# Attention with a routed expert gate: half of the projections placed in attention's first four chunks, and the gate cut into 128-token pieces

## The chip, the cores and the metric

One core of a Trainium2 chip runs the whole kernel in one launch. The metric is the device time in microseconds (us). Engines are named as in the profile: PE is TensorE (PEld its weight loads), DVE is VectorE, ACT is ScalarE, POOL is GpSimd, SP is SyncE, which here only issues transfers and waits. All data is float32.

## The reference

The input x has 2 batches of 2048 tokens with 256 features, 4096 tokens in all. It is normalised once, and both branches read the normalised rows.

```python
xn = layernorm(x)
# attention branch: 16 heads of 16, relative positions clipped to +-128
q, k, v = (heads(xn @ W.T + b) for W, b in ((Wq, bq), (Wk, bk), (Wv, bv)))
scores  = (q @ k.T + q . rel_k[clip(j - i, -128, 128) + 128]) / sqrt(16)
w       = softmax(scores)
s       = (w @ v + w . rel_v[clip(...) + 128]) @ Wo.T + bo
# expert branch: 8 experts (256 -> 1024 -> 256), one chosen for each token
e       = argmax(xn @ Wg + bg)
g       = silu(gelu(xn @ W1[e]) @ W2[e])
out     = x + s * g
```

## The kernel before

The work is done in three stages that follow each other on every engine; the order of the instructions within a stage is that of the source (`manual_schedule`), and a scheduler may place an instruction of a later stage earlier on an engine whose turn it is (loads of the attention stage stand among those of the expert stage on SP, for instance).

**Stage 1, up to 157 us: normalisation, routing, projections.** The tokens come in 8 blocks of 512 (`TB`, `NI = 8`). For each block, x is loaded, normalised on DVE, stored row-wise (`xn_d`, for the experts' gathers), and transposed on PE into `xnT`, which holds all 4096 tokens with the features on the partitions. `logits` multiplies by the router's weights. The projections are a list of 56 `pieces`, 7 per block: two of `queries` and two of `keys` (`project`, L272: two 128x512 products, an ACT activation that adds the bias, and a store to `q_d` or `k_d`), one `right_rows` (L294: the extra query row for keys beyond the right clip, from the products of the two q tiles, stored in `qx_d`), and two of `values_of` (L306: four 128x256 products, two DVE additions of the bias `bvl` into a buffer `vt` whose other columns hold ones, and a store to `v_d` after the second half). `right_rows` also stores a block of zeros `zq` into the other row of `qx_d` (L304). `work_pieces(n)` takes the next n pieces from the list; the calls stand where PE would wait for the normalisation (1 per block) and for the routing tables on DVE (2, and 13 at L496), and the rest, 30 and 3, at L523 and L542. Between the two the pieces are followed by L525 to L541, which need small loads that POOL issues at L507 to L512 (wo_t, relk_t, rvc, ones_r): ones are copied into the two key buffers, `into` is built, and L534 multiplies it with wo_t. Routing ends with `token` (L502): the list of tokens by expert, after which POOL gathers the rows of the first two tiles (`get_tokens`, L156) and SP loads the weights of the first two (`get_weights`, L143, L147).

**Stage 2, 157 to 430 us: the experts.** 19 tiles of 256 sorted tokens (`work`, L552): transposes, `hp` products (L583), gelu on ACT, `yp` products (L598), a store to `ys_d`. Weights and gathered rows are double-buffered.

**Stage 3, from 431 us: attention.** There are 2 batches x 4 groups of 4 heads x 16 chunks of 128 queries = 128 chunks; four chunks make a unit. Chunk n runs in `steps` of a written-out loop (L1093 to L1180). In each step PE gets score products: the band (keys within one chunk, `band_scores` L785), the relative scores of two later chunks (`rel_scores` L745), and the far keys of the unit before (`far_scores` L940), which exist from chunk 4 on. All of these take their PSUM tile from the pool `sps` with 5 buffers in turn; a drain (DVE for band and relative scores, ACT's exponential for far keys) frees it. After the drains come the "small" tasks that `at(k, ...)` has put into step k. The ones that matter here:

- `to_keys(n + 1)`, step 0: DVE L772, then on SP a store of the relative scores to DRAM (`qr_d`, L776) and a load back in skewed form (`r`, L778, 768 KB each). The band drains of chunk n + 1 (L801) read r; the last of them is followed by L813, one reduction per chunk, which I use as the chunk's mark.
- `band_weights(n - 1)`, steps 0 and 1: exponentials on ACT in r (L824), then on POOL a store to `w_d` (L837) and a load `wr` (L839).
- `turn_rel`, `turn_band`, `band_values`: transposes and products of the band's weights.
- `load_q`, `load_kv`: loads for the next unit (L657, L660) and the next head group (L670, L678), on SP.
- `gate(i, 0)` in step 3 of chunks 2 to 9: four indirect gathers (L692, POOL) bring the expert results of 512 tokens; `gate(i, 1)` in step 2 of chunks 4 to 11: tanh on ACT (L701), two POOL operations (L702, L703), and a store of the gate to `gate_d` on SP (L704).

SP is one queue in order: an instruction that waits holds everything behind it. So are POOL's and ACT's queues.

Of the kernel before, what the change touches and what calls it, by code (L numbers as in the profile page):

```python
# [8 lines left out]
F32 = mybir.dt.float32  # L9
I32 = mybir.dt.int32  # L10
AF = mybir.ActivationFunctionType
ALU = mybir.AluOpType
# [22 lines left out]
def attn_moe_gate_kernel(  # L35
# [60 lines left out]
    NI = T // TB  # L96

    xn_d = dram.tile([T, D], F32, name="xn_d")
    gate_d = dram.tile([P, NT * D], F32, name="gate_d")
    ys_d = dram.tile([NE * TE, D], F32, name="ys_d")  # L100
    q_d = dram.tile([D, T], F32, name="q_d")
# [6 lines left out]
    def load(name, shape, src, pool=const):  # L108
        t = pool.tile(shape, F32, name=name)
        nc.gpsimd.dma_start(out=t, in_=src)  # L110
        return t
# [9 lines left out]
    token = const.tile([P, NB], I32, name="token")  # L121
    expert = const.tile([P, NE], I32, name="expert")
    filled = const.tile([P, 1], I32, name="filled")
    vdiff = const.tile([P, 1], F32, name="vdiff")
    rel0 = const.tile([P, 1], F32, name="rel0")

# [9 lines left out]

    feeding = ExitStack()
    feed = feeding.enter_context(tc.tile_pool(name="feed", bufs=2, side="right"))

    def get_weights(i, pool):  # L140
        e = nc.sync.value_load(expert[0:1, i : i + 1], min_val=0, max_val=E - 1)
# [23 lines left out]
    with ExitStack() as own:  # L165
# [31 lines left out]
        for e in range(E):  # L197
            nc.vector.memset(rank[:, e : e + 1], float(E - e))
        wq_t = load("wq_t", [P, ND, D], wq.rearrange("(k p) m -> p k m", p=P), ln1)
        bq_t = load("bq_t", [P, ND], bq, ln1)  # L200
        wk_t = load("wk_t", [P, ND, D], wk.rearrange("(k p) m -> p k m", p=P), ln1)
        bk_t = load("bk_t", [P, ND], bk, ln1)
        rkc = load("rkc", [P, 2], relk_cols, ln1)
        wv_t = load("wv_t", [P, ND, D], wv.rearrange("(k p) m -> p k m", p=P), ln1)
        bvl = load("bvl", [P, HEADS, HD], bv.partition_broadcast(P), ln1)
# [50 lines left out]
        def logits(i):  # L256
            for t in range(i * CB, (i + 1) * CB):
                for k in range(ND):
                    nc.tensor.matmul(
                        plog[:, t, :],  # L260
                        lhsT=xnT[:, k, t * P : (t + 1) * P],
                        rhs=wg_t[:, k, :],
                        start=(k == 0),
                        stop=(k == ND - 1),
                    )

        qx_heads = qx_d.rearrange("(h two) t -> h two t", two=2)
        rights, qs = [], {}  # L270

        def project(i, w, a, bias, scale, dst, name):  # L272
            cols = slice(i * TB, (i + 1) * TB)
# [20 lines left out]
        def right_rows(i):  # L294
            cols = slice(i * TB, (i + 1) * TB)
            ps = pps.tile([HEADS, TB], F32, name="pp")
            for a in range(ND):
                nc.tensor.matmul(
                    ps, lhsT=rights[a], rhs=qs.pop((i, a)), start=(a == 0), stop=(a == ND - 1)
                )  # L300
            rt = prp.tile([HEADS, TB], F32, name="rt")
            nc.scalar.copy(rt, ps)
            nc.sync.dma_start(out=qx_heads[:, 1, cols], in_=rt)
            nc.sync.dma_start(out=qx_heads[:, 0, cols], in_=zq)  # L304

        def values_of(i, half):  # L306
            vt = vts[i % 2]
# [22 lines left out]


        pieces, later = [], []
        for i in range(NI):
            pieces += [(queries, i, 0), (queries, i, 1), (keys, i, 0), (keys, i, 1)]
            pieces.append((right_rows, i))
            later += [(values_of, i, 0), (values_of, i, 1)]
            if not 0 < i < 3:
                pieces, later = pieces + later, []

        def work_pieces(n):  # L340
            for what, *args in pieces[:n]:
                what(*args)
            del pieces[:n]

        take_stats(0)
        for i in range(NI):
            if i + 6 < NI:
                get_x(i + 6)
            if i + 1 < NI:
                take_stats(i + 1)  # L350
            normalise(i)
            if i == 0:
                nc.vector.tensor_scalar(bq_t, bq_t, HD**-0.5, None, ALU.mult)
                nc.vector.tensor_scalar(bk_t, bk_t, rkc[:, 0:1], None, ALU.add)

                nc.vector.tensor_tensor(
                    right, rkc[:, 1:2].to_broadcast([P, HEADS]),
                    rkc[:, 0:1].to_broadcast([P, HEADS]), ALU.subtract,
                )
                for a in range(ND):  # L360
                    r = ln1.tile([P, HEADS], F32, name=f"right{a}")
                    nc.gpsimd.affine_select(
                        out=r, in_=right, compare_op=ALU.is_ge, fill=0.0, base=a * P,
                        pattern=[[-HD, HEADS]], channel_multiplier=1,
                    )
                    nc.gpsimd.affine_select(
                        out=r, in_=r, compare_op=ALU.is_ge, fill=0.0, base=HD - 1 - a * P,
                        pattern=[[HD, HEADS]], channel_multiplier=-1,
                    )
                    rights.append(r)  # L370
                nc.gpsimd.memset(before, 1.0)
                nc.gpsimd.affine_select(
                    out=before, in_=before, compare_op=ALU.is_ge, fill=0.0, base=-1,
                    pattern=[[1, P]], channel_multiplier=-1,
                )
                nc.gpsimd.memset(ones, 1.0)
                nc.gpsimd.memset(zq, 0.0)
                nc.gpsimd.iota(
                    begin, pattern=[[TE, NE]], base=0, channel_multiplier=0,
                    allow_small_or_imprecise_dtypes=True,  # L380
                )
                nc.gpsimd.iota(place, pattern=[[1, P]], base=0, channel_multiplier=0)
                nc.gpsimd.iota(number, pattern=[[P, NT]], base=0, channel_multiplier=1)
                for vt in vts:
                    nc.gpsimd.memset(vt, 1.0)
            if i == 1:
                nc.vector.tensor_tensor(
                    bvl, bvl, rve[:, 0:1, :].to_broadcast([P, HEADS, HD]), ALU.add
                )
            if i > 0:  # L390
                logits(i - 1)
                work_pieces(1)
        logits(NI - 1)
        work_pieces(1)
        lnx.close()


# [122 lines left out]
        nc.gpsimd.memset(mass[:, MASS : MASS + 1], 1.0)  # L520
        for z in shifts:
            nc.gpsimd.memset(z, 0.0)
        work_pieces(len(pieces) - 3)  # L523
        for t in k_homes:
            nc.vector.tensor_copy(t, ones_r.to_broadcast([P, S]))  # L525

# [99 lines left out]
            _attention(own, again)  # L626

    def _attention(own, again):
        accp = own.enter_context(tc.tile_pool(name="sacc", bufs=1))
        gop = own.enter_context(tc.tile_pool(name="gout", bufs=2))  # L630
        gpp = own.enter_context(tc.tile_pool(name="gprod", bufs=1))
        kvp = own.enter_context(tc.tile_pool(name="kv", bufs=2))
        qrp = own.enter_context(tc.tile_pool(name="qr", bufs=2))
        rp = own.enter_context(tc.tile_pool(name="r", bufs=3))
        bandp = own.enter_context(tc.tile_pool(name="band", bufs=2))
        wrtp = own.enter_context(tc.tile_pool(name="wrt", bufs=1))
        smp = own.enter_context(tc.tile_pool(name="small", bufs=2))
        exps = own.enter_context(tc.tile_pool(name="exps", bufs=18))
        finp = own.enter_context(tc.tile_pool(name="fin", bufs=2))
        outp = own.enter_context(tc.tile_pool(name="outp", bufs=2))  # L640
        scr = own.enter_context(tc.tile_pool(name="scr", bufs=3, space=DRAM))
        sps = own.enter_context(tc.tile_pool(name="sps", bufs=5, space=PSUM))
        avps = own.enter_context(tc.tile_pool(name="avps", bufs=1, space=PSUM))
# [38 lines left out]
            groups[G] = {"kT": kT, "v": v}  # L682


        gates = {}

        def gate(i, stage):
            if stage == 0:
                yt = gates[i] = gop.tile([P, CB * D], F32, name="yt")
                for c in range(CB):  # L690
                    t = i * CB + c
                    nc.gpsimd.indirect_dma_start(  # L692
                        out=yt[:, c * D : (c + 1) * D],
                        out_offset=None,
                        in_=ys_d,
                        in_offset=bass.IndirectOffsetOnAxis(ap=slot[:, t : t + 1], axis=0),
                    )
                return
            yt = gates.pop(i)
            gt = gpp.tile([P, CB * D], F32, name="gt2")  # L700
            nc.scalar.activation(gt, yt, AF.Tanh, scale=0.5)  # L701
            nc.gpsimd.tensor_scalar(gt, gt, 0.5, 0.5, ALU.mult, ALU.add)  # L702
            nc.gpsimd.tensor_tensor(gt, gt, yt, ALU.mult)  # L703
            nc.sync.dma_start(out=gate_d[:, i * CB * D : (i + 1) * CB * D], in_=gt)  # L704


        def chunk_of(n):
# [352 lines left out]

        load_q(0)
        load_kv(0)
        for drain in [rel_scores(0, j) for j in range(HG)]:
            drain()
        to_keys(0)
# [27 lines left out]
        while n < NCH or values or any(queues) or n <= NCH + 2 * CB + 1:  # L1093
# [26 lines left out]
            if live and m == 6 and (G + 1) * NC < NCH:  # L1120
                at(0, load_kv, G + 1)
            if not again:
                if 2 <= n < 2 + T // TB:
                    at(3, gate, n - 2, 0)
                if 4 <= n < 4 + T // TB:
                    at(2, gate, n - 4, 1)
            Uf, stage = divmod(n - 2, CB)
            if 0 <= Uf - 2 < NU:
                at(0, finish, Uf - 2, stage)
# [11 lines left out]
            if 0 <= n - 1 < NCH:  # L1141
                for part in range(1, chunk_of(n - 1)["f1"] - chunk_of(n - 1)["f0"]):
                    at(min(4, steps - 1), turn_band, n - 1, part)
            for k in range(steps):
                drains, filled = [], []
                for j in range(HG):
# [122 lines left out]
```

## Time and profile before

| what | us |
|---|---|
| three runs | 2314.58, 2300.74, 2314.71 (median 2314.58) |
| the profiled execution | 2314.34 |
| its span, first to last instruction | 2312.6 |
| routing table `token` done (L502) | 95.85 |
| last projection piece / first expert product (L583) | 153.63 / 158.84 |
| end of the experts on PE / start of attention on PE | 429.43 / 431.44 |
| first product with far keys (L946), the start of chunk 4 | 491.64 |
| L813 of chunk 4 / 12 / 20 / 28 | 497.13 / 629.28 / 740.15 / 849.71 |

The profile's page gives busy time per engine, forty equal slices of the span (57.8 us each) with PE's granted clock, the costliest groups of instructions, and the transfers. In a timeline each row is a start, a length, and an instruction with its line and tiles; what stands in brackets is the idle time before it and what ended it. In the windows each row is a stretch, its length, the busy time and count on PE, PEld, DVE, ACT and POOL, the clock that PE was granted (1.00 is full speed), the share of the DMA engines in use, and GB/s. In a list of waits each row is a sum in us, how many times, and the longest.

### The profile page before, as it was taken

The numbers are of one execution on the slowest core, as the hardware profiler recorded it, in microseconds if no ns is written. First come the engines' busy times: TensorE is split into PE (matmuls) and PEld (weight loads), VectorE is DVE, ScalarE is ACT, GpSimd is POOL, SyncE is SP. The second block draws the span as 40 slices with busy tenths as digits, with TensorE's granted clock in tenths as the row PEclk, the third lists the DMA queues.
The fourth block names the chain that finished last, engine by engine and source line by source line (L and its number), as shares of the span: only waits on it lengthen the run. The fifth ranks groups of instructions, "written<-read, shape, count | busy, mean of one in ns | idle before, by whom it ended". The sixth has DMA issues, their size and how long they took to land. (4 is left out here: it accounts for less than half of the span.)

```text
span 2312.6 us, 58344 instructions
## 1 busy us (share of the span) xinstructions
PE 2204.5 (95%) x24314; PEld 1435.4 (62%) x24314; DVE 1065.3 (46%) x2688; ACT 1294.2 (56%) x2519; POOL 426.7 (18%) x587
## 2 busy tenths in 40 slices
PE   7999999788999999999999998899999999999996
PEld 5568888655565566666566565566556656656653
DVE  5421000244555555555455554455555555555542
ACT  2221111146666676666676666566667666666664
POOL 1201110045311111111111222211111111111221
PEclk9999999779999999999999999899999999999998
DMA  5646555477666766766676667566666666666652
GB/s 182 217 170 182 184 183 181 136 255 254 224 224 207 237 217 208 241 223 204 213 232 228 230 231 227 195 210 218 225 205 218 219 213 219 216 213 218 239 189 71
DMA packets 246802, 483.16 MB, mean 209 GB/s; under 512 B 16480, under 2 KB 194944, under 8 KB 246016
## 3 DMA queue, kind: packets, MB, share of 16 engines
q1 hardware_dynamic: 199648, 295.21, 38.8%
q0 software_dynamic: 41008, 178.84, 22.7%
q10 hardware_dynamic: 5872, 5.26, 0.7%
q8 instruction: 195, 3.19, 0.6%
q14 instruction: 79, 0.65, 0.1%
HBM read 244.89 MB, written 234.36 MB: 207 GB/s over the span
## 5 line engine op out<-in xcount | busy, mean ns | idle before, releaser
L956 ACT ACTIVATE ex<-sp 128x512 f32<-128x512 f32 x1728 | 893.3, 587 | 540.6 <-PE sp L946 420.9
L946 PE MATMUL sp<-qh,kT 32*128 32x512 f32 (+7 forms) x4096 | 766.0, 559 | 28.7 <-DVE stat L801 28.4
L801 DVE CUSTOM_DVE_ANT_0 r<-sp,r 128x384 f32<-128x384 f32 (+1 forms) x512 | 275.6, 539 | 615.7 <-PE sp L946 331.9
L791 PE MATMUL sp<-kT,qh 31*128 31x384 f32 (+1 forms) x1024 | 457.7, 533 | 0.0
L946 PEld LDWEIGHTS sp<-qh,kT 32*128 32x128 f32 (+1 forms) x4096 | 297.6, 184 | 220.7 <-issue 134.6
L966 PE MATMUL av<-ex,v 128*17 128x256 f32 (+2 forms) x7168 | 422.3, 371 | 0.0
L753 PE MATMUL sp<-relk_t,qh 32*128 32x256 f32 x1024 | 291.5, 412 | 13.8 <-DVE stat L801 10.8
L966 PEld LDWEIGHTS av<-ex,v 128*17 128x17 f32 (+1 forms) x7168 | 195.4, 99 | 173.6 <-issue 65.3
L824 ACT ACTIVATE r<-r,shift 128x384 f32<-128x384 f32 (+1 forms) x512 | 282.9, 613 | 10.0 <-DVE shift L813 10.0
L867 DVE COPY wt<-mp 128x512 f32<-128x512 f32 x368 | 242.6, 684 | 11.3 <-PE mp L865 6.2
L865 PEld LDWEIGHTS mp<-ident,r 128*128 128x128 f32 x1472 | 158.6, 142 | 143.0 <-issue 130.6
L839 POOL DMA_DIRECT2D wr<-w_d x128 | 97.8, 764 | 725.7 <-PE sp L946 167.0
L865 PE MATMUL mp<-ident,r 128*128 128x128 f32 x1472 | 220.4, 285 | 0.5 <-ACT r L824 0.5
L762 DVE COPY qr<-sp 128x512 f32<-128x512 f32 x256 | 175.4, 686 | 43.3 <-PE sp L946 34.7
L753 PEld LDWEIGHTS sp<-relk_t,qh 32*128 32x128 f32 x1024 | 172.2, 190 | 27.4 <-DVE stat L801 11.9
L888 PE MATMUL mp<-ident,wr 128*128 128x128 f32 x1024 | 157.9, 277 | 26.7 <-DVE qh L851 13.8
L837 POOL DMA_DIRECT2D w_d<-r x128 | 71.7, 560 | 514.3 <-ACT r L824 504.4
L590 ACT ACTIVATE hT<-hp 128x512 f32<-128x512 f32 x76 | 45.3, 597 | 215.7 <-PE hp L583 215.7
L791 PEld LDWEIGHTS sp<-kT,qh 31*128 31x128 f32 x1024 | 152.6, 187 | 4.0 <-issue 2.1
L888 PEld LDWEIGHTS mp<-ident,wr 128*128 128x128 f32 x1024 | 119.7, 142 | 48.8 <-DVE qh L851 25.9
L583 PE MATMUL hp<-xsT,w_t 128*128 128x256 f32 x608 | 134.4, 379 | 1.1 <-issue 1.1
L598 PE MATMUL yp<-w_t,hT 128*128 128x256 f32 x608 | 134.4, 379 | 0.0
(177 smaller groups left out, 1992.9 us busy)
## 6 DMA issues: line engine op xcount, KB each, us to landing
qr_d<-qr SPq DMA_DIRECT2D x128, 768.0 KB
r<-qr_d SPq DMA_DIRECT2D x128, 768.0 KB
w_d<-r POOLq DMA_DIRECT2D x128, 768.0 KB, 5.1
wr<-w_d POOLq DMA_DIRECT2D x128, 512.0 KB, 4.2
w_t<-in_w_dram SPq DMA_DIRECT2D x38, 1024.0 KB
ys_d<-ys ACTq DMA_DIRECT2D x19, 256.0 KB
v_d<-vt SPq DMA_DIRECT2D x8, 576.0 KB
v<-v_d SPq DMA_DIRECT2D x32, 144.0 KB
```

The lines of the kernel that those rows point to most:

```text
L583: nc.tensor.matmul(ps[:, m, :], lhsT=w1_t[:, k, (h + m) * P : (h + m + 1) * P], rhs=xsT[:, k, :], start=(k == 0), stop=(k == ND - 1),)
L753: nc.tensor.matmul(ps[:, 2 * x * P : 2 * (x + 1) * P], lhsT=ch["un"]["q"][32 * j : 32 * j + 32, chunk(ch["i"] + x)], rhs=relk_t[32 * j : 3 ...
L762: nc.vector.tensor_copy(ch["qr"][:, :, j, : 2 * P], ps.rearrange("p (x r) -> p x r", x=2))
L791: nc.tensor.matmul(ps[:, :bw], lhsT=ch["un"]["q"][32 * j : 32 * j + RIGHT, chunk(ch["i"])], rhs=ch["gr"]["kT"][32 * j : 32 * j + RIGHT, ch ...
L801: nc.vector.tensor_tensor_reduce(out=r, in0=ps[:, :bw], in1=r, scale=1.0, scalar=LOW, op0=ALU.add, op1=ALU.max, accum_out=stat[:, n, j, 0:1],)
L824: nc.scalar.activation(r[:, j, f0 * P : f1 * P], r[:, j, f0 * P : f1 * P], AF.Exp, bias=shifts[n % (2 * CB)][:, j, ONE : ONE + 1],)
L865: nc.tensor.transpose(ps[:, x, :], ch["r"][:, j, chunk(f0 + f)], ident)
L867: nc.vector.tensor_copy(dst, ps)
L888: nc.tensor.transpose(ps[:, jj, a, :], ch["wr"][:, 2 * pair + jj, chunk(a)], ident)
L946: nc.tensor.matmul(ps[:, at : at + e - a], lhsT=kT[32 * j : 32 * j + rows, chunk(kc)], rhs=q[32 * j : 32 * j + rows, a:e], start=True, sto ...
L956: nc.scalar.activation(exs[j][:, :n], ps[:, :n], AF.Exp)
L966: nc.tensor.matmul(un["av"][32 * j : 32 * j + cols, a:e], lhsT=v[:, kc, j, :cols], rhs=exs[j][:, at : at + e - a], start=False, stop=False ...
```

## The change

1. The pieces of stage 1 end after block 3: the list holds 28 of the 56. Everything up to the table product (L498) stays as it is, since the list is taken in order; L523 now takes 3 pieces and L542 the last two.
2. `xnT` of blocks 4 to 7 is stored to a new DRAM tensor `xT_d` (four stores of 512 KB on SP). The zero rows are stored in eight pieces at once in block 0.
3. At the start of attention `load_late` loads wq, wk, wv, bv and the four blocks of xT on ACT's queue, into buffers that the attention needs later (`gt`, `xo`, `sacc`), and adds to bvl on DVE. 28 `late_pieces` do what the pieces did, with PSUM tiles from `sps`, SBUF tiles from `exps`, and two `vt` buffers that POOL sets to one before each half. They are small tasks of chunks 0 to 3: two per step in chunks 0 and 1, one per step after that (10, 10, 5 and 3).
4. The gate takes 128 tokens at a time: one gather in step 3 of chunks 8 to 39, and tanh, two POOL operations and a 128 KB store in step 2 of chunks 9 to 40.
5. Pools are opened in another order, `gout` has 3 buffers and `gprod` 2; a quarter of the former size each.

```diff
+    NL = NI // 2
+    xT_d = dram.tile([(NI - NL) * P, ND * TB], F32, name="xT_d")
...
-            nc.sync.dma_start(out=qx_heads[:, 0, cols], in_=zq)
...
-        for i in range(NI):
+        for i in range(NL):
             pieces += [(queries, i, 0), (queries, i, 1), (keys, i, 0), (keys, i, 1)]
             pieces.append((right_rows, i))
             later += [(values_of, i, 0), (values_of, i, 1)]
...
+                for n in range(NI):
+                    nc.sync.dma_start(out=qx_heads[:, 0, n * TB : (n + 1) * TB], in_=zq)
...
+            if i > NL:
+                n = i - 1 - NL
+                nc.sync.dma_start(
+                    out=xT_d[n * P : (n + 1) * P, :].rearrange("p (k t) -> p k t", k=ND),
+                    in_=xnT[:, :, (i - 1) * TB : i * TB],
+                )
...
-        work_pieces(len(pieces) - 3)
+        work_pieces(len(pieces) - 2)
...
+        exps = own.enter_context(tc.tile_pool(name="exps", bufs=18))
         accp = own.enter_context(tc.tile_pool(name="sacc", bufs=1))
-        gop = own.enter_context(tc.tile_pool(name="gout", bufs=2))
-        gpp = own.enter_context(tc.tile_pool(name="gprod", bufs=1))
+        outp = own.enter_context(tc.tile_pool(name="outp", bufs=2))
+        gop = own.enter_context(tc.tile_pool(name="gout", bufs=3))
+        gpp = own.enter_context(tc.tile_pool(name="gprod", bufs=2))
+        vtp = own.enter_context(tc.tile_pool(name="vt", bufs=2))
...
+        def load_late():
+            tiles = [outp.tile([P, ND, D], F32, name=n) for n in ("gt", "gt", "xo", "xo")]
+            for t, w in zip(tiles, (wq, wk, wv)):
+                nc.scalar.dma_start(out=t, in_=w.rearrange("(k p) m -> p k m", p=P))
+            bvl = tiles[3][:, 0, :].rearrange("p (h x) -> p h x", x=HD)
+            nc.scalar.dma_start(out=bvl, in_=bv.partition_broadcast(P))
+            nc.vector.tensor_tensor(
+                bvl, bvl, rve[:, 0:1, :].to_broadcast([P, HEADS, HD]), ALU.add
+            )
+            xT = accp.tile([P, NC, D], F32, name="sacc").rearrange("p c d -> p (c d)")
+            xT = xT[:, : (NI - NL) * ND * TB].rearrange("p (i k t) -> p i k t", k=ND, t=TB)
+            for n in range(NI - NL):
+                nc.scalar.dma_start(
+                    out=xT[:, n, :, :],
+                    in_=xT_d[n * P : (n + 1) * P, :].rearrange("p (k t) -> p k t", k=ND),
+                )
...
+        def late_rows(i, n, a):
+            ps = sps.tile([P, TB], F32, name="sp")
+            for k in range(ND):
+                nc.tensor.matmul(
+                    ps, lhsT=w[:, k, a * P : (a + 1) * P], rhs=late["xT"][:, i, k, :],
+                    start=(k == 0), stop=(k == ND - 1),
+                )
+            t = exps.tile([P, TB], F32, name="ex")
+            nc.scalar.activation(t, ps, AF.Identity, bias=bias[:, a : a + 1], scale=scale)
+            nc.sync.dma_start(out=dst[a * P : (a + 1) * P, cols], in_=t)
...
+        def late_values(i, half):
+            vt = vtp.tile([P, NG, 2, HG, VW], F32, name="vt")
+            nc.gpsimd.memset(vt, 1.0)
+            ps = sps.tile([P, 2, NG, HG, HD], F32, name="sp")
...
+        late_pieces = []
+        for i in range(NI - NL):
+            late_pieces += [(late_rows, i, 0, 0), (late_rows, i, 0, 1)]
+            late_pieces += [(late_rows, i, 1, 0), (late_rows, i, 1, 1)]
+            late_pieces += [(late_right, i), (late_values, i, 0), (late_values, i, 1)]
...
-        def gate(i, stage):
+        def gate(t, stage):
             if stage == 0:
-                yt = gates[i] = gop.tile([P, CB * D], F32, name="yt")
-                for c in range(CB):
-                    t = i * CB + c
-                    nc.gpsimd.indirect_dma_start(
+                gates[t] = gop.tile([P, D], F32, name="yt")
+                nc.gpsimd.indirect_dma_start(
...
+        if not again:
+            load_late()
...
-                if 2 <= n < 2 + T // TB:
-                    at(3, gate, n - 2, 0)
-                if 4 <= n < 4 + T // TB:
-                    at(2, gate, n - 4, 1)
+                if 2 * CB <= n < 2 * CB + NT:
+                    at(3, gate, n - 2 * CB, 0)
+                if 2 * CB + 1 <= n < 2 * CB + 1 + NT:
+                    at(2, gate, n - 2 * CB - 1, 1)
...
+            if not again and n < CB:
+                for k in range(steps):
+                    for _ in range(2 if n < 2 else 1):
+                        if late_pieces:
+                            at(k, *late_pieces.pop(0))
```

## The prediction

> **What bounds the kernel now.** In the page's forty slices TensorE (PE) is 90% busy or more almost everywhere, so time comes from stretches where it is idle, clocked low, or doing work that could stand elsewhere. First PE's timeline between routing and experts (start, us, what):
>
> ```profile
> 106.11 3.60 PE L276 MATMUL pp<-xnT,wq_t 128*128 128x512 f32 x8
> 109.54 3.60 PE L276 MATMUL pp<-xnT,wk_t 128*128 128x512 f32 x8
> 113.06 1.89 PE L298 MATMUL pp<-q,right 128*16 128x512 f32 x4
> 114.89 3.72 PE L312 MATMUL pp<-wv_t,xnT 128*128 128x256 f32 x16
> 118.44 3.60 PE L276 MATMUL pp<-xnT,wq_t 128*128 128x512 f32 x8
> ...
> 157.18 0.60 PE L565 MATMUL xp<-ident,xs 128*128 128x128 f32 x4
> 158.84 7.14 PE L583 MATMUL hp<-xsT,w_t 128*128 128x256 f32 x32 [1.05 <-issue]
> ```
>
> No idle time: one block of 512 tokens costs 12.33 us (106.11 to 118.44), four of them 49.3, and the first expert product waits for the last. Next the windows of the attention's start and of its run-in (us, length, busy PE, PEld, DVE, ACT, POOL, granted clock, DMA share, GB/s):
>
> ```profile
> 431.40:444.90 13.50, 5.42 (x33) 4.01 (x33) 3.92 (x9) 0.60 (x1) 0.47 (x1) 0.59 0.51 172
> 444.90:491.80 46.90, 41.62 (x202) 25.63 (x204) 22.54 (x63) 9.74 (x19) 14.38 (x19) 0.50 0.72 250
> ...
> 540.40:546.40 6.00, 6.00 (x68) 3.10 (x68) 0.55 (x2) 2.09 (x4) 3.50 (x5) 0.50 0.77 249
> 546.40:552.00 5.60, 5.60 (x75) 2.91 (x70) 2.35 (x6) 2.70 (x7) 1.69 (x2) 1.00 0.81 266
> ```
> ```profile
> 497.10:629.30 132.20, 116.72 (x1405) 69.68 (x1404) 62.74 (x147) 82.41 (x157) 65.31 (x63) 0.92 0.74 248
> 629.30:740.10 110.80, 109.00 (x1394) 67.77 (x1392) 59.63 (x150) 74.88 (x149) 18.12 (x28) 0.98 0.63 213
> 740.10:849.70 109.60, 107.47 (x1418) 67.67 (x1416) 61.22 (x154) 75.12 (x149) 16.19 (x25) 1.00 0.69 225
> ```
>
> Chunks 0 to 3 (431.4 to 491.6, 60.2 us) run at half clock: 41.6 us busy there is 20.8 at full. They are paced by a loop: to_keys of the next chunk stands behind this chunk's first band drain on DVE, which waits for r. The waits of 429 to 492 say so; those of 497 to 629 name the second loss:
>
> ```profile
> DVE r L801 <- DMA r<-qr_d: 30.5, 5, 7.6
> ```
> ```profile
> SPq L704 <- POOL gt L703: 52.3, 8, 9.1
> SPq L778 <- DMA qr_d<-qr: 39.6, 8, 9.6
> ```
>
> Eight chunks (from one L813 reduction to the eighth after it) take 132.2 us where the gate runs and 110 where it doesn't: the gate's excess is 22.
>
> **The change, part by part.** The sum is against the profiled execution, 2314.3 us (span 2312.6, and 1.7 around it); the median shown, 2314.6, is the same number.
>
> *Out of the prologue: 28 pieces, 49.3 us of PE.* All of it lay on the path, but not all is won, since what was hidden under it comes due: L534, which folds a column into wo_t, needs the ones rows and rvc.
>
> ```profile
> 104.30 0.60 POOL L110 DMA_DIRECT2D ones_r<-in_ones_rows_dram  x1
> ...
> 143.99 2.35 DVE L525 COPY kT<-ones_r 128x2048 f32<-128x2048 f32 x2
> 146.26 0.15 DVE L527 TENSOR_TENSOR vdiff<-rvc 128x1 f32<-128x1 f32 x1
> 146.51 0.62 DVE L529 COPY into<-vdiff 32x1 f32<-32x1 f32 x4
> ```
>
> ones_r takes 7.0 us to land: 111.3. Then 2.35 of copies, 0.9 to the end of `into`: L534 can start at 114.7. In the built order two value pieces stand behind it: 1.89 + 3.56 = 5.45 us at full clock. PE will have idled since 102 (three value pieces after the table), and here a rule counts against the change. After an idle gap of 7.2 us the row above shows 6.0 us of fully busy PE at 0.50 before the clock returns; the Trainium skill, "TensorE: Matmul & The Clock Gate", Part 1, gives one busy window of about 3.4 us. By the row the loss is 6.0/2 = 3.0, by the page 1.7; I take the row. PE ends at 114.7 + 5.45 + 3.0 = 123.1, and the experts' first product follows 1.5 later as before (157.35 to 158.84): 124.6 for 158.84, **-34.2**. The weights (4 MB issued at 87.5 to 90.2) and the gathers (issued 96.3 to 101.2, 4.7 to land) are there by then. Bounds: -31 if wo_t or rvc land late, -37 if the clock stays up.
>
> *Small moves in the prologue, counted as nothing.* The eight zq stores go to SP after the memset at 15.35; 8 x 0.41 holds SP to 18.7, and the x load behind them went out at 18.92 anyway. Four xT_d stores (2 MB) go out among the xn_d and q_d stores from 45 on, where the DMA share is 0.30 to 0.49; uncovered they would cost 8 us at 250 GB/s. Two vt memsets (0.5 us each by L385's rows) stand ahead of the gathers on POOL and wait for the last stores of the projection tiles, issued by 86.7; POOL sleeps until 96.34. If those stores were late, the gather would be.
>
> *Into chunks 0 to 3.* ACT issues eight loads (2.9 MB), and DVE's first instruction, the addition to bvl, waits for the fourth: four issues of 0.39, 896 KB at 250 GB/s (3.6), 0.8 for landing (768 KB of qr_d take 3.87, 3.1 of it bytes): 6.0. Behind it on DVE are the relative-score drains (2.48), L772 (0.43), and so the qr_d store: 9.4 after the start for 4.8 before. This store shares the engines with what is left of xT. "DMA: Bandwidth & Descriptors", section on queues, rings and completion order, says that each engine takes turns between the queues that have work; taken literally 3.9 becomes 7.8. The nearest row, a qr_d store behind kT and v loads (757.30, its r at 762.86), took 5.6; I take 5.6. Then r at 4.4: it lands at 19.5 for 12.9, until when PE can do only two pieces, because the fifth score buffer back is the band's, which DVE holds.
> From there PE is the limit: 26 pieces, 45.9; its own 20.8 at full clock; 3.0 for a cold start. The value pieces add a chain: their memset stands on POOL behind w_d (5.1 to land) and wr of the chunk before, DVE waits for the memset, and the band drains, wt copies and PE's buffers wait behind DVE. In chunk 1 I get 2 us of PE stall, in chunk 3 about 5: 7. Chunk 4 starts at 19.5 + 45.9 + 20.8 + 3.0 + 7 = 96.2 for 60.2: **+36**. The 28 late stores (6.5 MB) beside the 11.7 MB that stretch moves make 18.2 MB in 77 us, 237 GB/s, no more than now. Bounds: +13 if every idle moment is filled (60.2 less 3.2 and 20.8 at full clock leaves 36.2 for 49.3), +63 if nothing overlaps (49.3 + 6.6 + 7).
>
> *The gate.* Chunks 4 to 11 lose the big gate: -22, of which I count 19, as part may be the run-in itself. In 32 chunks come one gather (1.25 of POOL with its gap), 0.35 of ACT, 0.9 of POOL, and a store that SP waits for. No row shows one; it lies between 0 and the present 2.8 per chunk. POOL reaches it after wr. In steady chunks wr + 1.7 comes before the next qr_d is ready three times in four, and the r loads have 0 to 4 us to spare: I take 0.3 per chunk, +10, near the low end. **-9**.
>
> Sum: 2314.3 - 34.2 + 36 - 9 = **2307**.
>
> **Rivals.**
> *The gaps really are free.* PE fills them and only 13 us are left: 2314.3 - 34.2 + 13 - 9 = 2284. For it: PE is at half clock there, dense pieces would raise it. Against it: in-order score buffers.
> *The first chunks add up.* Pieces and round trips in series, +63: 2334. For it: the same five buffers serve late pieces, band and relative scores. Against it: ACT drains the late ones at once.
> *The gate's price is per visit, not per byte* (the one on the other side). SP stops at each gate store until POOL has it; if 32 stops cost 2.8 each as the eight do, +90 for the 10 above: 2387. It makes the kernel slower at all from 0.53 per chunk, by 1% from 1.25. For it: 52 us of SP waits on POOL. Against it: POOL's part falls from 8.4 to 2.2 us per chunk.
> *No gain in the prologue*: another transfer, weights or gather, holds the experts at the old time; about 2341. The landings above speak against it.
>
> **How the numbers follow.** The main case 0.52 (its own range 2291 to 2322), free gaps 0.20, series 0.14, per visit 0.10, no gain 0.04. Tails of two in ten left out: 2278 to 2343. Faster by over 1% (about what a measurement here can tell; below 2291): most of the second case and the edge of the first, 0.23. Slower by over 1% (above 2338): the gate case, no gain, a third of the series, 0.19. The rest, 0.58.
>
> **What would show it.** First L583 product near 125. PE idle from 102 to 114.7, then low clock. Attention's start to the first far product (L946) 96 us, clock mostly 1.00 there; chunks 4 to 11 at 113; later gate chunks at 14.0 each. It is wrong if the first four chunks take under 75 or over 115 us, or if SP's waits for POOL in chunks 9 to 40 move the r loads.

## The result, and the profile after

| | median, us | before on the same chip | ratio, 95% interval |
|---|---|---|---|
| the changed kernel | 2312.45 (20 runs) | 2314.64 | 0.9985 (0.9964 to 1.0007) |
| once more, with the experiments | 2309.81 (22 runs) | 2316.84 | 0.9964 (0.9943 to 0.9984) |
| the kernel before against itself | 2315.40 (14 runs) | 2318.91 | 0.9993 (0.9972 to 1.0014) |

The ratios are taken over the executions in the faster of two states and are not quite the quotients of the medians. The first two, weighted by their intervals, make 0.9974 (0.9959 to 0.9989): 6 us of 2315, and no change by the bound of one per cent. Behind it stand four large terms that nearly cancel. With two profiles of each kernel the budget is (us; c4 is the L813 reduction of chunk 4, which is L915 in the changed kernel, and so on; the third row is called "start to far" below):

| stretch | before | after | difference (mean) | predicted |
|---|---|---|---|---|
| start to first expert product | 158.8, 159.5 | 126.3, 127.0 | -32.5 | -34.2 |
| experts, up to attention's start on PE | 272.6, 272.6 | 272.6, 272.7 | 0 | 0 |
| attention's start to first far product | 60.2, 61.3 | 102.0, 100.4 | +40.5 | +36 |
| from there to c4 | 5.5, 6.7 | 5.5, 6.3 | 0 | 0 |
| c4 to c12 (the big gate's chunks) | 132.2, 132.1 | 109.3, 107.9 | -23.5 | -19 |
| c12 to c40 (the rest of the small gates) | 384.4, 387.2 | 395.0, 393.5 | +8.5 | +10 |
| c40 to the end | 1298.9, 1294.5 | 1300.4, 1301.2 | +4 | 0 |

The last row is within what two profiles of one kernel differ by (4.4). The first row moves as much with the execution: the six profiles of this document with the changed kernel's prologue have their first expert product at 122.7 to 127.4, the three with the old one at 158.8 to 162.8, and the two means differ by 34.7. In the changed kernel's timeline, PE between the table product and the experts, and then DVE in the same time:

```profile
98.29 6.99 PE L318 MATMUL pp<-wv_t,xnT 128*128 128x256 f32 x24
116.98 3.75 PE L551 MATMUL tps<-wo_t,into 128*128 128x256 f32 x8 [11.70 <-DVE into L546]
120.53 4.32 PE L318 MATMUL pp<-wv_t,xnT 128*128 128x256 f32 x16
...
126.29 3.07 PE L600 MATMUL hp<-xsT,w_t 128*128 128x256 f32 x13 [1.01 <-DVE xsT L586]
```
```profile
113.57 2.36 DVE L542 COPY kT<-ones_r 128x2048 f32<-128x2048 f32 x2 [7.50 <-DMA ones_r<-in_ones_rows_dram]
...
116.10 0.62 DVE L546 COPY into<-vdiff 32x1 f32<-32x1 f32 x4
```

Before, PE had no gap here. Now it idles 11.7 us until `into` is built, and behind the gap the fold takes 3.75. The windows of that place, of the attention's first four chunks and of the eight-chunk stretches (columns as before the change: us, PE, PEld, DVE, ACT, POOL, clock, DMA share, GB/s):

```profile
114.70:120.70 6.00, 3.72 (x9) 3.03 (x10) 3.15 (x10) 0.00 (x0) 0.00 (x0) 0.50 0.00 0
120.70:126.30 5.60, 4.59 (x22) 3.70 (x20) 3.18 (x9) 0.00 (x0) 0.73 (x1) 0.89 0.00 0
```
```profile
398.90:420.00 21.10, 11.20 (x32) 5.50 (x33) 3.73 (x7) 1.00 (x2) 0.00 (x0) 0.60 0.65 211
...
476.30:493.50 17.20, 15.06 (x102) 8.74 (x100) 6.63 (x21) 3.88 (x7) 3.05 (x5) 1.00 0.70 242
493.50:500.90 7.40, 6.71 (x62) 4.66 (x62) 4.02 (x9) 2.61 (x5) 1.19 (x2) 0.54 0.51 179
```
```profile
506.30:615.60 109.30, 107.15 (x1405) 65.43 (x1404) 58.44 (x148) 77.01 (x154) 23.33 (x34) 0.98 0.70 232
615.60:723.80 108.20, 107.90 (x1394) 67.56 (x1392) 59.66 (x152) 77.42 (x158) 36.46 (x53) 1.00 0.72 238
723.80:838.50 114.70, 111.21 (x1418) 69.02 (x1416) 61.01 (x154) 77.47 (x157) 34.03 (x49) 0.97 0.71 229
```

PE is at full clock and seldom idle from 420 to 493 (the windows left out have 15.74 of 15.90, 22.06 of 22.50 and 17.90 of 17.90 busy), where it was at half clock before; most of what is lost lies in the first 21 us. PE's rows there:

```profile
411.05 2.07 PE L855 MATMUL sp<-relk_t,qh 32*128 32x256 f32 x4 [9.40 <-DVE qr L864]
413.05 6.59 PE L729 MATMUL sp<-sacc,gt 128*128 128x512 f32 x8
419.57 1.12 PE L855 MATMUL sp<-relk_t,qh 32*128 32x256 f32 x4
420.63 3.70 PE L729 MATMUL sp<-sacc,gt 128*128 128x512 f32 x8
```

PE idles 9.4, until DVE drains the relative scores, which stand behind the addition to bvl. Then the first two late pieces take 6.59 at the slow clock, the next two 3.70; r of chunk 0 is used at 421.6. Chunks 4 to 11 run like any others. Chunks 20 to 27 have become slower than chunks 12 to 19, with PE at 0.97. Among the waits of 399 to 501, the first line below is the value pieces behind POOL's memset, the second the addition to bvl; then SP's waits for the gate in chunks 4 to 11, the counterpart of the 52.3 in 8 of before:

```profile
DVE vt L767 <- POOL vt L754: 17.9, 2, 11.7
...
DVE xo L711 <- DMA xo<-in_bv_dram: 12.3, 1, 12.3
```
```profile
SPq L806 <- POOL gt L805: 18.8, 3, 6.9
```

### The profile page after: what moved, and what is told of

The parts are those of the page before. It is cut to its first block, busy times and chain, and to the rows that moved or that the text cites. A ratio compares the mean times of both kernels' runs of the same rounds, so it can differ in the third digit from the quotient of the medians.

```text
span 2311.1 us, 58525 instructions
## 1 busy us (share of the span) xinstructions
PE 2205.3 (95%) x24314; PEld 1432.7 (62%) x24314; DVE 1063.1 (46%) x2689; ACT 1295.6 (56%) x2543; POOL 443.2 (19%) x643
## 5 line engine op out<-in xcount | busy, mean ns | idle before, releaser
L1048 PEld LDWEIGHTS sp<-qh,kT 31*128 31x128 f32 (+1 forms) x4096 | 298.0, 184 | 207.0 <-issue 136.1
```

The costliest lines, as they stand in the source:

```text
L1048: nc.tensor.matmul(ps[:, at : at + e - a], lhsT=kT[32 * j : 32 * j + rows, chunk(kc)], rhs=q[32 * j : 32 * j + rows, a:e], start=True, sto ...
```

## Experiments

The theory is the budget: three separate terms (prologue, first chunks, gate), each set by the wait that the prediction names. The rivals are named with each run. "Changed" is the changed kernel; where a run is compared with it, the two ratios to the kernel before are divided (the changed kernel's with its pooled 0.9974).

**The projections alone, and the gate alone.**

```diff
 e1: the changed kernel with the gate of before
-                if 2 * CB <= n < 2 * CB + NT:
-                    at(3, gate, n - 2 * CB, 0)
+                if 2 <= n < 2 + T // TB:
+                    at(3, gate, n - 2, 0)
 (exps 16 buffers for 18)
 e2: the kernel before with the gate of the changed one
```

> The projections are moved as in the change, the gate stays as it was (512 tokens per visit, chunks 2 to 11); the exps pool has 16 buffers for 18, to make room. Theory (three separate terms): the first expert product near 126 for 158.8 (-32.5), attention's start to the first far product near 102 for 60.2 (+42), maybe 2 to 4 more because the first gate visits stand in chunks 2 and 3; chunks 4 to 12 again near 130 to 132, later stretches as before; about 2322 to 2328. Rival (the 23 us that chunks 4 to 11 lost came from the warm, dense start and not from the gate): chunks 4 to 12 near 110, and the whole near 2302.

Measured: 2325.04, ratio 1.0079 (1.0056 to 1.0102). First expert product 124.1; start to first far product 100.2; c4 to c12 125.8; c12 to the end 1694.4 for 1683.3 and 1681.7 before.

> The gate alone is cut to 128 tokens in chunks 8 to 40, the projections stay in the first stage. Theory: nothing changes up to chunk 4 (first expert product 158.8, start to first far product 60); chunks 4 to 12 near 110 to 113 for 132, chunks 12 to 40 together 11 to 13 longer than before; about 2303 to 2306. Rival (the gain of chunks 4 to 11 came from the warm start): chunks 4 to 12 stay near 130, and with the price of the small gates the whole is near 2325.

Measured: 2303.28, ratio 0.9969 (0.9949 to 0.9990). First expert product 162.8; start to far 60.5; c4 to c12 111.4; c12 to c40 393.2.

The rival falls: without the moved projections the small gate takes c4 to c12 from 132 to 111, and with them it takes it from 126 to 109. So 17 to 21 of the 23.5 are the gate's; the moved projections alone bring 6. Two more things stand in these runs. Each half alone also has the late loss: c12 to c40 is 393.4 in the first and 393.2 in the second, as with both (395.0 and 393.5), for 384.4 and 387.2 before. And the whole runs do not add up: +18 for the one and -7 for the other (ratios times 2315) make +11, and both together are -6, a difference of 17 beside intervals of about 5, 5 and 3.5. The profiles, one execution each, do add up (spans +10 and -15 to the mean of before, -3 for both together), so the difference lies in no stretch that they show; it stays open.

**The fold** (the product of wo_t with `into`, L534 before, L551 in the changed kernel). The six small loads are issued in block 0, and DVE prepares the fold before the last 13 pieces that lie under the routing.

```diff
+                wo_t = load("wo_t", ...)   # with bo_t, relk_t, rvd, rvc, ones_r, in block 0
...
         nc.vector.tensor_copy(filled, ends[:, E - 1 : E])
+        for t in k_homes:
+            nc.vector.tensor_copy(t, ones_r.to_broadcast([P, S]))
+        nc.vector.tensor_tensor(vdiff, rvc[:, 1:2], rvc[:, 0:1], ALU.subtract)
+        for j in range(HG):
+            nc.vector.tensor_copy(into[...], vdiff[...])
         work_pieces(13)
```

> The changed kernel, with the six small loads (wo_t, bo_t, relk_t, rvd, rvc, ones_r) issued in block 0 and with DVE's copies of ones and the construction of the folded column ahead of the last 13 pieces that lie under the routing. Theory (the idle stretch before the fold is the wait for ones_r and the copies): PE's gap of 11.7 before the fold goes, its clock stays up, the first expert product comes near 112 to 114 for 126.3, all later marks move rigidly with it; about 2298 to 2300. Rival (the token gathers or the weights are as late as the fold): the first expert product stays above 120, and the whole gains under 6.

Measured: 2291.11, ratio 0.9916 (0.9888 to 0.9945); against the changed kernel 0.994 (0.991 to 0.997). PE's timeline in its profile:

```profile
106.10 2.04 PE L552 MATMUL tps<-wo_t,into 128*128 128x256 f32 x8
107.97 3.62 PE L320 MATMUL pp<-wv_t,xnT 128*128 128x256 f32 x16
...
113.03 2.21 PE L601 MATMUL hp<-xsT,w_t 128*128 128x256 f32 x9 [1.01 <-DVE xsT L587]
```

No idle time stands before the fold, and the first expert product stands at 113.0 for 126.3. So the fold held the experts back to 126; by 113 the weights and gathers were there. The same two rows also measure the cold clock: the fold and the two value pieces take 2.04 and 3.62 here, 3.75 and 4.32 behind the gap, 2.4 more.

**Half as much moved.** Only blocks 6 and 7 move (14 pieces, one per step).

```diff
-    NL = NI // 2
+    NL = NI - 2
...
-                    for _ in range(2 if n < 2 else 1):
+                    for _ in range(1):
```

> The changed kernel with only blocks 6 and 7 moved (14 pieces, one per step of chunks 0 to 2), blocks 0 to 5 in the first stage. Theory (the wait for the fold ends at 114.7 in any case, so 24.6 more of pieces fill PE's idle 11.7 and the slow clock behind it; in the first chunks about 27 of pieces and gaps fit beside the attention's own work): first expert product 137 to 139, attention's start to first far product 72 to 78 for 102; about 2299, 10 less than the changed kernel. Rival (each piece costs the same in either place, and the start of the attention is set by its loads): first expert product above 145, or the first chunks above 82, and within 4 of the changed kernel.

Measured: 2297.33 (6 runs), ratio 0.9903 (0.9866 to 0.9939); against the changed kernel 0.993 (0.989 to 0.997). First expert product 138.3, start to far 71.9, both as the theory had them (72 to 78 for the second). 14 pieces, 24.6 of PE, come back into the prologue and cost 12 there, because they fill the wait for the fold; in the first chunks they save 29.

**The head of the attention.** First, only the addition to bvl moves on DVE, to just ahead of the first value piece.

> The changed kernel with the addition to bvl moved on DVE from the head of the attention to just ahead of the first late value piece; nothing else. Theory (DVE's 12.3 wait for bv delays the drains, the qr_d store and r of chunk 0): r of chunk 0 lands near 416 for 421.5, PE's gap of 9.4 shrinks to about 2 to 4, attention's start to first far product 96 to 98 for 102. Rival (the loads of xT, not the order on DVE, set when r lands): r lands within 2 of 421.5, and 101 to 102.

Measured: 2306.29, ratio 0.9970 (0.9951 to 0.9989); against the changed kernel 1.000 (0.997 to 1.002). Start to far 101.4. The rival's numbers came: DVE's order does not set r. SP's timeline, first the changed kernel (attention's start 398.9), then this run (395.3): the store of the relative scores and the load of r of chunk 0.

```profile
413.28 0.56 SPq L878 DMA_DIRECT2D qr_d<-qr  x1
417.15 0.40 SPq L880 DMA_DIRECT2D r<-qr_d  x1
```
```profile
400.44 0.56 SPq L879 DMA_DIRECT2D qr_d<-qr  x1
414.07 0.40 SPq L881 DMA_DIRECT2D r<-qr_d  x1
```

The store goes out 9 us earlier after the start (5.1 for 14.4), but takes 13.6 for 3.9, since it now runs beside the 2.9 MB of late loads. r is first used 23.3 after the start for 22.7. So the same lateness comes by either of two ways, through the wait for bv or through a store that runs beside the loads. That the volume of the loads sets it is not shown: the run with half as much moved loads 1.0 MB less, and its r is used at 21.7. PE's first idle time is 7.7 here, and what ends it is the landing of the first block of xT.

Second, the loads and pieces are rearranged: wq and the first block of xT first, bv last, four pieces ahead of chunk 0's first band scores, all value pieces after the row pieces. The run includes the early fold and the gate's store on POOL's queue.

```diff
         to_keys(0)
+        if not again:
+            for _ in range(4):
+                what, *args = late_pieces.pop(0)
+                what(*args)
```

> The changed kernel with the early fold preparation, with the gate's store from POOL's queue, and with the head of the attention rearranged: wq and the first block of xT loaded first, bv last and its addition just ahead of the first value piece, four late pieces ahead of chunk 0's first band scores, and all value pieces after the row pieces. Theory: first expert product near 113; PE has work from 408 or so less the 13 of the fold on, instead of idling 9.4; attention's start to first far product 88 to 94 for 102; about 2281 in all. Rival (the four pieces ahead take the score buffers and PE's turn from the band, and delay what they save; the value pieces at the end pile up on POOL and DVE): 100 or more, and about 2288.

Measured: 2291.26 (6 runs), ratio 0.9880 (0.9838 to 0.9922); first expert product 113.7, start to far 91.9. In the windows of its first chunks PE has work 7 us after the start, and from 396 on it is busy and at full clock:

```profile
386.40:396.00 9.60, 6.11 (x20) 3.35 (x21) 3.49 (x6) 0.00 (x0) 0.00 (x0) 0.51 0.68 225
396.00:472.70 76.70, 75.18 (x292) 38.81 (x292) 26.68 (x74) 20.90 (x34) 9.61 (x16) 0.97 0.71 239
```

r is hardly earlier than it was (used 21.1 after the start), yet 6 to 9 us are won (91.9 here, 95.4 in the next run, for 101.2): what costs is PE's idle time ahead of the first pieces, 3.5 here for 9.4, more than r itself. The expected total, 2281, was missed, and 2291 is nearer to the rival's 2288: c4 to c12 took 116.0.

> The kernel with the early fold and four pieces ahead of chunk 0, four blocks moved, with the gate's store back on SP's queue. In the two profiles with four blocks moved and the store on POOL's queue, chunks 4 to 12 took 114.3 and 116.0 for 107.8 to 109.3 with the store on SP; chunks 12 to 40 took 386.7 and 393.1 for 393 to 395. Theory (the store on POOL costs 6 to 8 in chunks 4 to 12, where w_d and wr stand behind it): chunks 4 to 12 near 108, the first chunks 92, chunks 12 to 40 near 394, the whole near 2286. Rival (the 116 came from the dense start, not from the store): chunks 4 to 12 near 116 again, and 2292 or more.

Measured: 2290.11, ratio 0.9908 (0.9880 to 0.9936); start to far 95.4, c4 to c12 114.1, c12 to c40 397.1. The 114 came back with the store on SP, so the dense start does hand a few us on to the chunks behind it: PE idles 4.0 just behind c4, before a product with far keys. But the store on POOL's queue has a price of its own: with the ordinary start it too takes c4 to c12 to 114.3 (the run further down), there with a gap of 3.3 behind c11. The run before this one has both gaps, 2.3 behind c4 and 3.3 behind c11. The total, 2290, lies between the theory's 2286 and the rival's 2292.

> The kernel with the early fold, the gate's store on POOL's queue and four pieces ahead of chunk 0, with only blocks 6 and 7 moved. Theory (there PE is busy from end to end in the first chunks, so a piece costs the same 1.76 in either place): first expert product near 138, attention's start to first far product 67 to 70 for 91.9, and within 4 of the version with four blocks, about 2288. Rival (14 pieces fit into the gaps that the first chunks have anyway, 60.2 without any piece): 60 to 63 for the first chunks, and 2281.

Measured: 2295.28 (6 runs), ratio 0.9902 (0.9866 to 0.9937); first expert product 139.6; start to far 79.6, which neither expected. The mean clock in that stretch is 0.74: with 14 pieces, four of them ahead, chunks 2 and 3 are left without any, PE gets gaps (2.8 at 453) and the clock drops again. In the whole it is as fast as the version with 28 pieces (0.9880), within the intervals.

**The price of the small gates.** With the changed kernel once more, on the same chip:

> The changed kernel once more, for a second profile and a ratio on the chip of the following runs. Expected: ratio to the kernel before 0.997 to 1.000; the marks up to chunk 4 within 2 of the first profile (126.3, 398.9, 500.9). Open is the stretch from chunk 12 to 40, 395.1 in the first profile and 384.4 before: if it is the price of the small gates it is again above 392; if single profiles scatter by that much, it is anywhere between 385 and 396.

Measured: as in the table at the top; c12 to c40 393.5.

> The kernel before once more, unchanged, for a second profile. Chunks 12 to 40 took 384.4 in its one profile and 393 to 398 in those of the changed kernel and of all its variants but one (386.7 with the gate's store on POOL's queue). If that is the change's late loss, this profile is again below 388; if one profile scatters by 10 there, it may lie above 390. Ratio 0.998 to 1.002.

Measured: c12 to c40 387.2, ratio 0.9993. So the late loss of some 9 is no scatter; four more versions with the same gate have 393.4 to 397.1 there.

> The changed kernel, with the store of the small gate issued from POOL's queue, so that SP never waits for POOL. Theory (what the small gates cost is SP's stop, which moves the qr_d stores and r loads behind it): chunks 12 to 40 take near 384 for 395, the whole is 10 less, about 2302. Rival (the price is POOL's time, the gathers or the transfers themselves): chunks 12 to 40 stay within 3 of 395, the whole within 3 of the changed kernel; slower if POOL, waiting for its own product, holds back wr.

```diff
-            nc.sync.dma_start(out=gate_d[:, t * D : (t + 1) * D], in_=gt)
+            nc.gpsimd.dma_start(out=gate_d[:, t * D : (t + 1) * D], in_=gt)
```

Measured: 2297.82, ratio 0.9943 (0.9919 to 0.9966); against the changed kernel 0.997 (0.994 to 1.000); c12 to c40 386.7, c4 to c12 114.3. The theory's 384 nearly came in this profile (of an execution of 2317, one of the longest of the run); in all 7 are won (0 to 14), with some 6 lost in c4 to c12. But the other two versions with this store, the rearranged start with 28 and with 14 pieces, have 393.1 and 396.0 from c12 to c40.

> The changed kernel without any gate visit: no gather, tanh, product or store; the end of the attention reads another tensor in its place, so the output leaves the gate out. Theory (32 small gates cost 10 together): about 10 less than the changed kernel on the same chip, chunks 12 to 40 near 385. Rival (they cost nothing that can be measured, and 395.1 against 384.4 was scatter or comes from something else in the change): within 4 of the changed kernel.

Measured: 2315.62, ratio 0.9989 (0.9967 to 1.0010), for 2309.81 of the changed kernel on the same chip; c12 to c40 397.6. Without any gate it is not faster. The two runs have to be read together. SP's timeline at the loads of a head group, first before, then in the changed kernel; then the changed kernel's PE and one window:

```profile
750.12 3.44 SPq L678 DMA_DIRECT2D v<-v_d  x4
757.30 0.52 SPq L776 DMA_DIRECT2D qr_d<-qr  x1
762.86 0.37 SPq L778 DMA_DIRECT2D r<-qr_d  x1
```
```profile
738.09 0.34 SPq L806 DMA_DIRECT2D gate_d<-gt  x1
738.49 1.85 SPq L688 DMA_DIRECT2D kT<-k_d  x4
...
742.42 0.77 SPq L878 DMA_DIRECT2D qr_d<-qr  x1
751.92 0.37 SPq L880 DMA_DIRECT2D r<-qr_d  x1
```
```profile
757.12 2.08 PE L1048 MATMUL sp<-qh,kT 32*128 32x512 f32 x4 [2.81 <-DVE stat L903]
```
```profile
757.00:763.00 6.00, 5.88 (x68) 3.16 (x72) 1.29 (x5) 2.09 (x4) 0.58 (x1) 0.50 0.54 199
```

SP stands at the gate's store until 738.1; the loads of the next head group go out only then, and the store of the relative scores, 0.1 behind them, takes 9.5. Before, 3.7 lay between and it took 5.6. PE idles 2.8 for r and then runs 6 us at half clock: 5.8 lost. A like gap of 4.4 follows at 856, after a stop of SP for POOL of 10.0. Every one of the seven profiles with small gates and the store on SP has both gaps, of 1.8 to 4.6 us; none of the three with the store on POOL has one above 1.2 there. That mechanism is the one that the prediction feared, and its sign of being wrong: SP's waits for POOL do move the r loads. It is the small gate's doing and not that of the moved projections or of the pools' order, for the gate alone, with the pools in the order of before, has both gaps (1.8 and 3.4) and the same two long stretches (114.1 from c20 to c28 and 115.6 from c28 to c36, for 114.7 and 116.2 in the changed kernel and 109.6 each before).

Without any gate the loss moves elsewhere. POOL's and SP's timelines, first without the gate, then the changed kernel at the same chunk (w_d and wr are a chunk's weights going to DRAM and back, 768 and 512 KB):

```profile
678.02 0.38 SPq L857 DMA_DIRECT2D r<-qr_d  x1
```
```profile
678.19 0.54 POOL L916 DMA_DIRECT2D w_d<-r  x1 [7.15 <-ACT r L903]
687.71 0.76 POOL L918 DMA_DIRECT2D wr<-w_d  x1 [8.99 <-DMA w_d<-r]
```
```profile
678.48 0.38 SPq L880 DMA_DIRECT2D r<-qr_d  x1
```
```profile
677.57 0.59 POOL L939 DMA_DIRECT2D w_d<-r  x1 [5.02 <-ACT r L926]
682.62 0.77 POOL L941 DMA_DIRECT2D wr<-w_d  x1 [4.47 <-PE sp L1048]
```

Without the gate, r and w_d start within 0.2 us, share the engines, and w_d needs 9.0; the wr load behind it then leaves beside the next qr_d store (687.63), and PE idles 3.45 for wr at 691.9. In the changed kernel the two starts are 0.9 apart and wr leaves 5.1 after w_d. At the same chunk the kernel before has a gap of 1.5. A reading that fits, but that no edit tested, is that a stretch with some 70% of the engines' time taken depends on how SP's and POOL's round trips happen to fall, and that the gate's visits shift this. The gate's own work has no price that could be measured (the ratio of with to without is 0.9975, plus or minus 0.003). Why the two runs without gates from chunk 12 on lie at 393 to 398, and the kernel before at 384 to 387, stays open: both have the pools in the new order, which moves every buffer, and that was not tried by itself.

## Why the prediction was right, point by point

- **Out of the prologue: -34.2, measured -32.5** (-34.7 over all nine profiles). Shown by the early fold. The terms: `into` was done at 116.7 for 114.7, because the routing table came 2.7 later in that profile (98.5 for 95.85) and ones_r landed 6.6 after its issue at 107.0. The slow clock cost 2.4, between the estimate of 1.7 worked out from the Trainium skill's window ("TensorE: Matmul & The Clock Gate", Part 1) and the 3.0 from the row of before: "I take the row" was 0.6 too much.
- **Small moves counted as nothing:** the later routing table is not their doing. The projections alone and the run with the late addition to bvl have the same prologue and the table at 96.2 and 96.4; the gate alone has the old prologue and the table at 99.1. So they cost nothing that can be told from this scatter.
- **First four chunks: +36, measured +40.5.** The mechanism, two pieces until r and then PE as the limit, was right; four terms of the sum were not. bv landed 11.1 after the start for 6.0, the loads having gone out only 2.4 after it; the store behind it took 3.9 for 5.6 (beside the loads, with the addition late, 13.6, where the literal turns gave 7.8), and r was used at 22.7 for 19.5. The step "DVE's first instruction waits, and so the qr_d store is late" is what the trace shows, but it is not what keeps r late: with that wait removed r is as late. "Its own 20.8 at full clock", half of the busy time at half clock, was too small: from r on it is 29.3 of time on PE (each product counted by how far it moves PE's end) beside the pieces' 46.6 (predicted 45.9), some 3.1 of it by the slow clock of the last 7.4 us; that leaves 26.2. Counted so, between half clock (before, from 444.8) and full clock (here, up to 493.5), a relative product went from 0.31 to 0.18 and a transpose from 0.25 to 0.14, a band product of 384 columns only from 0.54 to 0.36. Of the 3.0 for a cold start nothing fell behind r: the slow clock lay ahead of it. Against it, PE's stall by the chain behind the value pieces was 2.8 for 7: DVE did wait 17.9 for POOL's memset, but PE had enough in its other buffers.
- **The gate: -9, measured -23.5 + 8.5 = -15.** The reserve of 3 for a run-in was not needed (-23.5 of the excess of 22, and -21 with the gate alone). The +10 has the right size by two profiles of each kernel, and the gaps at 754 and 856 come from SP's stop, as named, so that the prediction's own sign of being wrong, SP's waits moving the r loads, was there. It is not the price of 32 visits at 0.3 each: it sits in two collisions, and taking all the gates away gives nothing back.
- **The sum** is right in part by luck: the three terms were off by +1.7, +4.5 and -6, and -7.2 met -7.
- **Rivals.** "The gaps really are free" fell in the changed kernel as written; the rearranged head shows part of it (start to far 91.9 and 95.4), and with 14 pieces, 24.6 of PE, the gaps take up more than half: 71.9 to the 60.2 of none. "In series" (+63) and "per visit" (+90) fell; "no gain in the prologue" fell.

The 49.3 us of moved pieces won 32.5 and cost 40.5. The change as a whole lives from the gate; moving the projections loses 8 in these profiles (6 with the prologue over all nine), because in the old place they covered PE's wait for the fold and in the new one PE has to wait for their loads. Both can be mended: with the fold early the kernel is 0.8% faster than before, with half as much moved 1.0%, and with the fold early, the start rearranged and the store on POOL 1.2%, all within each other's intervals.

## What to carry to other kernels

Work that is moved out of a stretch gives back only what nothing else then waits for: list what was hidden under it (here a 7 us landing and 3 us of copies) and bring that forward first. In the new place count the loads that the moved work needs before counting idle time on the compute engine; a gap that is a wait for transfers is not a place for work that brings 2.9 MB of transfers along. Where transfers keep the engines 70% busy, as here, shifting an issue queue by a few us can cost or save as much as the work that was edited, so judge an edit by removing its cost, not by a wait that carries its name.

## What the runs showed of the hardware

A gap of 2.8 us on PE was enough for 6 us at a granted clock of 0.50 (757 to 763), as long as behind the gap of 7.1 in the kernel before (540.4 to 546.4); the price of a short wait was thus doubled. Still shorter gaps had the same sequel: 2.1 us at 489 (clock 0.54 from 493.5 to 500.9) and, with the gate alone, 1.8 us at 751 (0.50 from 752.9 to 759.3). Behind a gap of 1.5 us in the kernel before, the clock stayed at 1.00 (764.1 to 771).

The same 768 KB store took 3.9 us with no load beside it, and behind the 2 x 4 loads of a head group 5.6, 7.5 and 9.5, when 3.7 (before), 1.6 (the gate's store on POOL) and 0.1 us (the changed kernel) lay between; beside 2.9 MB on another queue it took 13.6.

And one kernel's executions spread over 36 us (2292 to 2329 in 60 runs of the kernel before), while the stretches of two profiles of one kernel agreed to 4.4 us or better.
